# Two-layer graph network with attention: residual adds on VectorE, later signs, earlier reciprocals, a later row of means

## Chip, cores and metric

The kernel runs on one core of a Trainium2 chip. The metric is the device time in microseconds of one execution. All arithmetic is float32.

## What is computed

The reference takes x (16 batches of 1024 nodes with 256 features) and an adjacency matrix of 1024 x 1024, and applies two layers, each followed by a layer norm over the features. The second layer is the one that the change concerns:

```python
x = layernorm(x + L0(x, adj, ...))        # two matrix products with batch norms
# L1, per batch, fea = x transposed (C x N)
c = mean(x over features)                  # one number per node
A = abs(abs(sigmoid(c[None,:] - c[:,None]) - 0.5) - 0.5) * 2.0
Wg = adj * (A + A.T) * 0.5
g = relu(einsum('cn,nm->cm', fea, Wg) * para)
q = heads(g.T);  k, v = heads(x @ kv_w)    # 4 heads of 64
attn = softmax(q @ k.T * scale)
x = layernorm(x + attn @ v)
```

The abs(abs()) expression is computed by the kernel as 1 + tanh(-|d|/2) on the difference d of two nodes' means. For odd rows it takes tanh(-d/2) and sets the sign bit, which gives the same.

## The kernel before

The first layer takes the time up to about 820 us of the profile. From there `fast()` runs the second layer as one software pipeline over the 16 batches. It is cut into 256 attention steps, 16 to a batch. A step computes the scores of two blocks of keys for a pair of heads and 512 queries (`scores`, L771), their exponentials on ScalarE (`exps`, L783), adds these into a running sum on VectorE (`sums`, L789 and L792), and multiplies them with the values (`attend`, L807). After the last key block ScalarE and VectorE put the two halves of the product together (`ot`, L818 and L819), and SyncE stores it to DRAM.

Between groups of four steps stand the other pieces of work, each a small function that issues instructions on several engines in program order:

- `dens` (L834, L836): TensorE sums the running sums `acc` over partitions into `pd`; ScalarE copies that to `dt`. `recips` (L845, L847): TensorE transposes `dt` into `pr`, VectorE takes reciprocals into `RD`.
- `fetch_o` loads the stored attention output back in 32 x 32 blocks (`ob`, L860); `finish_a` transposes it on VectorE (L876), multiplies by the reciprocals (L880) and adds the residual `x1` (L885), on GpSimd for all batches but the last. `finish_s` takes layer-norm statistics of the sum on VectorE (`st_z`, `mv_z`) and the scale on GpSimd (`rs_z`, `nm`). `finish_b` applies them on ScalarE (L901) and stores the rows.
- For the next batch but one: `load`, `bn2_q` (GpSimd, L603), `rows` (VectorE, L607 and L608), `ln1_a` (statistics), `ln1_b` (VectorE, L628), `put_x1`, `get_x1` and `x1_v` (a transpose by way of DRAM), `means` (VectorE, L667 and L669), and `crow`, which spreads the row of means over all partitions: TensorE transposes it (`pc`, L684), ScalarE copies it (L686), SyncE writes it to DRAM and reads it back into 128 partitions (L687, L688).
- For the next batch: `gate` (ScalarE's abs and tanh into `wg`, L696 to L701; VectorE's sign, L698, and the product with the adjacency, L705), `keys`, `values` and `graph` (TensorE, L720, L731, L745) and `queries` (L753, L754).

A table `at` says in which half step-group each piece is issued. `arrange` puts the pieces of one half in order: pieces with short TensorE work are spread among the long ones (`keys`, `values`, `graph`), others go in by the rank in the tuple `order`, and gates are spread among the rest or put ahead. The first `sums` of a group is issued after the last short piece (`behind`). Each engine works through its own queue in this order, and an instruction that waits holds up all behind it.

Of the kernel before, what the change touches and what calls it, by code (L numbers as in the profile page):

```python
# [11 lines left out]
OP = mybir.AluOpType  # L12
# [10 lines left out]
def gnn_norm_attention_kernel(  # L23
# [16 lines left out]
    nc = tc.nc  # L40
    B, N, C = x.shape
# [82 lines left out]
    with ExitStack() as l0:  # L124
# [32 lines left out]
        with ExitStack() as ph1:  # L157
# [9 lines left out]
            for i in range(0, NT, 2):  # L167
                t = hp.tile([P, 2, N], F32, tag="h", name=f"A{i}")
# [22 lines left out]
            KB = FB // P  # L191
# [6 lines left out]
            for h in range(NH):  # L198
                rows = range(h * KB, (h + 1) * KB)
# [243 lines left out]
        with ExitStack() as ph2:  # L443
# [74 lines left out]
            for k, pair in enumerate(pairs):  # L518
# [4 lines left out]
                if not ahead:  # L523
                    for j in range(LDP):
                        load(0, j)
                    for j in range(LDP, NT // 2):
                        t = accp.tile([P, 2, FB], F32, tag="acc", name=f"first{j}")
# [17 lines left out]
    def ln_stats(sm, r, name):  # L545

        n = r.shape[1]
        mv = sm.tile([P, n, 2], F32, tag="mv", name=f"mv_{name}")
        for a in range(n):
            st = sm.tile([P, 6], F32, tag="st", bufs=2, name=f"st_{name}_{a}")  # L550
            nc.vector.bn_stats(st, r[:, a, :])  # L551
            nc.vector.bn_aggr(mv[:, a, :], st)
        rs = sm.tile([P, n], F32, tag="rs", name=f"rs_{name}")
        rsqrt(rs, mv[:, :, 1], EPS)
        return mv, rs
# [4 lines left out]
    def fast():  # L560
      with ExitStack() as fx:
# [15 lines left out]
        x1s, x1Ts, css, crows, mvs, wgs = {}, {}, {}, {}, {}, {}  # L577
# [113 lines left out]
        def wg_a(b, i):  # L691
            t = wgp.tile([P, N], F32, tag="wg", name=f"wg_{b}_{i}")
            wgs[b, i] = t
            if i % 2:

                nc.scalar.activation(t, crows[b], AF.Tanh, bias=hcs[b][:, i : i + 1], scale=-0.5)  # L696
                ti = t.bitcast(mybir.dt.int32)
                nc.vector.tensor_scalar(ti, ti, -(2**31), None, op0=OP.bitwise_or)  # L698
            else:
                nc.scalar.activation(t, crows[b], AF.Abs, bias=css[b][:, i : i + 1], scale=-1.0)  # L700
                nc.scalar.activation(t, t, AF.Tanh, scale=-0.5)  # L701

        def wg_b(b, i):
            t = wgs[b, i]
            nc.vector.scalar_tensor_tensor(t, t, 1.0, adj_sb[:, i, :], op0=OP.add, op1=OP.mult)  # L705

        def gate(b, i):
# [88 lines left out]
        def by_pe(b, hf):  # L796
            return b == B - 1 and hf == NH - 1
# [41 lines left out]
        R = {}  # L839
        KB = FB // P  # L840
# [24 lines left out]
        def finish_a(b, j):  # L865
            hf, k = divmod(2 * j, KB)
            pool_r = (rp, "r") if b < B - 1 else (x1p, "x1")
            r = pool_r[0].tile([P, 2, C], F32, tag=pool_r[1], name=f"r_{b}_{j}")
            if by_pe(b, hf):
                p = ps_t.tile([P, 2, C], F32, tag="t", name="pf")  # L870
                for a in range(2):
                    for pair in range(NP):
                        nc.tensor.transpose(p[:, a, ts(pair, P)], OT[b, hf, pair][:, ts(k + a, P)], ident)
            else:
                p = r
                nc.vector.transpose(  # L876
                    r.rearrange("p a c -> p (a c)"), OB.pop((b, j)).rearrange("p a c -> p (a c)")
                )
            rd = RD[:, b * NT + 2 * j : b * NT + 2 * j + 2, :].rearrange("p a h -> p (a h)")
            nc.vector.tensor_mul(  # L880
                r.rearrange("p a (h d) -> p (a h) d", h=HEADS),
                p.rearrange("p a (h d) -> p (a h) d", h=HEADS),
                rd.unsqueeze(2).to_broadcast([P, 2 * HEADS, HD]),
            )
            (nc.gpsimd if b < B - 1 else nc.vector).tensor_add(r, r, x1s.pop((b, j)))  # L885
            R[b, j] = r

        def finish_s(b, j):
            r = R[b, j]
            mv, rs = ln_stats(sm, r, f"z{b}_{j}")  # L890
            nm = sm.tile([P, 2], F32, tag="nm", name=f"nm_{b}_{j}")
            for a in range(2):
                nc.gpsimd.tensor_scalar(
                    nm[:, a : a + 1], mv[:, a, 0:1], rs[:, a : a + 1], -1.0, op0=OP.mult, op1=OP.mult
                )
            R[b, j] = (r, rs, nm)
# [42 lines left out]
        def put(w, t, f, *a):  # L939
            at.setdefault(w * NC + t, []).append((f, a))  # L940
# [4 lines left out]
        for b in range(B):  # L945

            for hf in range(NH):
                t = (hf + 1) * (NC // NH)
                put(b, t, dens, b, hf)
                put(b, t + 1, recips, b, hf)  # L950
                for k in range(KB // 2):
                    put(b, t + k, fetch_o, b, hf * (KB // 2) + k)
                    put(b, t + 1 + k, finish_a, b, hf * (KB // 2) + k)
                    put(b, t + 1 + k, finish_s, b, hf * (KB // 2) + k)
                    late = 0 if b == B - 1 else 1
                    if b == B - 1 and hf == 0:
                        late = NC - t - 2 - k
                    put(b, t + 2 + k + late, finish_b, b, hf * (KB // 2) + k)
            if b == 0:
                continue  # L960

            put(b - 2, 2, begin, b)
            for j in range(NT // 2):
                put(b - 2, j, load, b, j)
                put(b - 2, j + 1, bn2_q, b, j)
                put(b - 2, j + 2, rows, b, j)
                put(b - 2, j + 2, ln1_a, b, j)
                put(b - 2, j + 3, ln1_b, b, j)
                if b == 1:
                    put(b - 2, j + 4, x1_t, b, j)  # L970
                    continue
                put(b - 2, j + 3, put_x1, b, j)
                put(b - 2, 5 + j // 2 * 2, get_x1, b, j)
                put(b - 2, min(6 + j, NC), x1_v, b, j)
            put(b - 2, NC - 2, means, b)
            put(b - 2, NC - 1, crow, b)

            i = 0
            for t, n in enumerate(WG):
                for i in range(i, i + n):  # L980
                    put(b - 1, t, gate, b, i)
                i += 1
            kv = [(keys, (b, c, h)) for h in range(NH) for c in range(CT)]
            kv += [(values, (b, j)) for j in range(0, NT, 2)]
            for t, n in enumerate(KV):
                for _ in range(n):
                    f, a = kv.pop(0)
                    put(b - 1, t, f, *a)
            m = 0
            for t, n in enumerate(QG):  # L990
                for m in range(m, m + n):
                    put(b - 1, NC - len(QG) + t, graph, b, m)
                m += 1
# [3 lines left out]
        nsteps = B * NS  # L997


        order = (dens, recips, x1_t, finish_a, fetch_o, finish_b, x1_v, rows, ln1_a, ln1_b, put_x1, get_x1, finish_s, means, load, crow)  # L1000
        rank = {f: k for k, f in enumerate(order)}
        short = (dens, recips, x1_t, crow)

        def is_short(fa):
            f, a = fa
# [2 lines left out]
        long = (keys, values, graph)  # L1008

        def spread(few, many):  # L1010

            res, done = [], 0
            for k, fa in enumerate(few):
                upto = len(many) * (k + 1) // (len(few) + 1)
                res += many[done:upto] + [fa]
                done = upto
            return res + many[done:]

        def arrange(pieces):
            first = [fa for fa in pieces if fa[0] is dens]  # L1020
            gates = [fa for fa in pieces if fa[0] is gate]
            many = [fa for fa in pieces if fa[0] in long]
            first += [fa for fa in pieces if fa[0] is bn2_q]
            few = [fa for fa in pieces if fa not in first + gates + many]
            few.sort(key=lambda fa: rank.get(fa[0], len(rank)))
            few_pe = [fa for fa in few if is_short(fa)]
            order = spread(many, few_pe) if len(many) < len(few_pe) else spread(few_pe, many)
            if few_pe and many and order[0][0] in long:
                order.remove(few_pe[0])
                order.insert(0, few_pe[0])  # L1030

            for fa in few:
                if not is_short(fa):
                    at_ = 0
                    for k, o in enumerate(order):
                        if o[0] in rank and rank[o[0]] <= rank.get(fa[0], len(rank)):
                            at_ = k + 1
                    order.insert(at_, fa)
            if any(fa[0] is graph for fa in many):
                return first + gates + order  # L1040
            return first + spread(order, gates)

# [22 lines left out]
        def gate0(i):  # L1067
            wg_a(0, i)
            wg_b(0, i)
# [81 lines left out]
        )  # L1151

    flag = fast()


# [153 lines left out]
```

## Time and profile before

| | |
|---|---|
| median of 3 runs | 2532.7 us (2531.0 to 2536.48) |
| profiled execution | span 2531.8 us, the run 2533.6 us |
| TensorE clock granted | 0.995 |
| one batch in the steady part | 105.1 us |
| GpSimd's residual adds, L885 | 60, 1.27 us each |
| VectorE's sign operations, L698 | 64, 0.69 us each |

The profile gives the busy time of each engine over the span. The wait lists say, for an engine, which instruction waited, what ended the wait, how long in all, how often, and the longest. In a timeline each row has the start, the duration, the engine, the line and tile, and in brackets the idle time of the engine just before and what ended it. PE is TensorE, DVE VectorE, ACT ScalarE, POOL GpSimd, SP SyncE.

### The profile page before, as it was taken

How to read it: one execution, taken by the hardware profiler on the slowest of the kernel's cores; microseconds unless marked ns; L12 is line 12 of the kernel's file. 1: busy time of each engine (PE TensorE's matmuls, PEld its weight loads, DVE VectorE, ACT ScalarE, POOL GpSimd, SP SyncE). 2: the span in 40 equal slices, each digit the busy share in tenths (PEclk: the TensorE clock that was granted, in tenths of full speed). 3: DMA queues.
4: the chain of work that ended last, by engine and by line, in shares of the span. 5: the costliest groups of instructions: out<-in, count | busy, mean ns of one | idle time of the engine just before them, and what ended most of it. 6: DMA issues, size and time to landing. Idle time of an engine off the chain costs nothing.

```text
span 2531.8 us, 33526 instructions
## 1 busy us (share of the span) xinstructions
PE 2445.6 (97%) x12341; PEld 1025.0 (40%) x12341; DVE 1791.6 (71%) x2716; ACT 1037.6 (41%) x1325; POOL 786.3 (31%) x766
## 2 busy tenths in 40 slices
PE   8999999998998999999999999999999999999997
PEld 4444444443443433343343433434334343343432
DVE  5545554556767677877878778787787887878657
ACT  2000000004453446364563645636446364463644
POOL 2222322232565222331423314233142331423122
PEclk9999999999999999999999999999999999999999
DMA  3122212230885223333333233332333324323111
GB/s 133 67 89 94 100 68 93 88 126 28 289 312 183 59 46 72 84 71 79 74 73 87 64 85 72 70 88 63 83 75 69 88 63 89 71 67 88 26 42 44
DMA packets 545770, 225.71 MB, mean 89 GB/s; under 512 B 388680, under 2 KB 533696, under 8 KB 538432
## 3 DMA queue, kind: packets, MB, share of 16 engines
q1 hardware_dynamic: 545600, 223.50, 33.2%
q8 instruction: 99, 1.62, 0.3%
q14 instruction: 71, 0.58, 0.1%
HBM read 129.52 MB, written 93.91 MB: 88 GB/s over the span
## 4 chain that ended last, share of the span: by engine, by line
PE 41%; DVE 19%; issue 5%; ACT 5%; DMA 3%; POOL 2%; SPq 1%; DVEq 0%; POOLq 0%; ACTq 0%
PE s L771 11%; PE o L807 10%; PE pg L745 10%; DVE acc L792 8%; PE po L483 7%; DVE wg L705 2%; DVE x L628 2%; DMA yt<-yT 1%; PE pv L731 1%; PE pd L834 1%; ACT wg L700 1%; ACT wg L696 1%; POOL yt L603 1%; ACT wg L701 1%; DVE st_z L551 1%
## 5 line engine op out<-in xcount | busy, mean ns | idle before, releaser
L783 ACT ACTIVATE e<-s 128x1024 f32<-128x1024 f32 x512 | 496.5, 1022 | 619.1 <-PE s L771 565.0
L792 DVE TENSOR_TENSOR acc<-acc,e 128x1024 f32<-128x1024 f32 x384 | 508.5, 1324 | 79.9 <-ACT e L783 50.4
L771 PE MATMUL s<-qT,kT 64*64 64x512 f32 x4096 | 492.1, 595 | 18.6 <-ACT e L783 17.9
L807 PE MATMUL o<-e,v 64*64 64x512 f32 x4096 | 494.7, 589 | 0.0
L745 PE MATMUL pg<-wg,x 128*128 128x512 f32 x960 | 427.2, 595 | 0.0
L603 POOL TENSOR_TENSOR yt<-yt,stq 128x512 f32<-128x512 f32 x120 | 169.4, 1412 | 459.2 <-DMA yt<-yT 304.9
L807 PEld LDWEIGHTS o<-e,v 64*64 64x64 f32 x4096 | 160.9, 133 | 288.6 <-issue 271.1
L771 PEld LDWEIGHTS s<-qT,kT 64*64 64x64 f32 x4096 | 147.7, 133 | 314.5 <-issue 266.6
L745 PEld LDWEIGHTS pg<-wg,x 128*128 128x128 f32 x960 | 177.6, 190 | 219.7 <-issue 211.3
L885 POOL TENSOR_TENSOR r<-r,x 128x512 f32<-128x512 f32 x60 | 76.4, 1274 | 451.5 <-issue 380.3
L102 ACT COPY u<-pa 128x512 f32<-128x512 f32 x15 | 8.8, 586 | 475.3 <-PE pa L307 475.3
L705 DVE SCALAR_TENSOR_TENSOR wg<-wg,adj_sb 128x1024 f32<-128x1024 f32 x128 | 157.6, 1251 | 7.7 <-ACT wg L701 7.5
L307 PE MATMUL pa<-AhT,x 128*128 128x512 f32 x360 | 161.8, 592 | 0.0
L720 PE MATMUL pk<-x1T,kvw 128*128 128x512 f32 x256 | 118.4, 606 | 1.3 <-DVE x1T L664 1.3
L731 PE MATMUL pv<-kvw,x1T 128*128 128x256 f32 x512 | 117.1, 382 | 0.0
L338 PE MATMUL ph<-agg,SW 128*128 128x512 f32 x240 | 112.8, 592 | 0.0
L731 PEld LDWEIGHTS pv<-kvw,x1T 128*128 128x128 f32 x512 | 96.0, 190 | 31.5 <-issue 16.2
L307 PE MATMUL pa<-T,sx 128*128 128x512 f32 x240 | 107.9, 592 | 0.0
L307 PEld LDWEIGHTS pa<-AhT,x 128*128 128x128 f32 x360 | 68.4, 190 | 86.1 <-issue 86.1
L483 PE MATMUL po<-hL,SV 128*128 128x512 f32 x224 | 98.4, 592 | 0.0
L819 DVE TENSOR_TENSOR ot<-o,ot 128x512 f32<-128x512 f32 x64 | 44.0, 687 | 74.7 <-ACT ot L818 74.7
L467 ACT ACTIVATE hL<-hL,t,s 128x512 f32<-128x512 f32 x112 | 79.7, 802 | 25.0 <-DMA hL<-h 25.0
(195 smaller groups left out, 3035.8 us busy)
## 6 DMA issues: line engine op xcount, KB each, us to landing
h<-hT SPq DMA_DIRECT2D x28, 1024.0 KB, 4.4
hL<-h SPq DMA_DIRECT2D x28, 1024.0 KB, 9.6
x<-in_x_dram SPq DMA_DIRECT2D x16, 1024.0 KB, 7.3
yT<-y SPq DMA_DIRECT2D x64, 256.0 KB, 2.6
out_dram<-r SPq DMA_DIRECT2D x64, 256.0 KB, 2.4
xr<-in_x_dram SPq DMA_DIRECT2D x62, 256.0 KB, 3.0
o<-ot SPq DMA_DIRECT2D x62, 256.0 KB, 2.3
ob<-o SPq DMA_DIRECT2D x248, 64.0 KB, 2.2
```

What stands on the lines that cost most here:

```text
L307: nc.tensor.matmul(p, xs[n][:, k, :], bs[n][:, k, :], start=(k == 0), stop=(k == KN - 1))
L338: nc.tensor.matmul(p, ws[n][:, ts(f, P)], bs[n], start=True, stop=True)
L483: nc.tensor.matmul(p, ws[n][:, k, :], bs[n][:, k, :], start=(k == 0), stop=(k == KF - 1))
L603: nc.gpsimd.tensor_tensor(y, y, sc, op)
L705: nc.vector.scalar_tensor_tensor(t, t, 1.0, adj_sb[:, i, :], op0=OP.add, op1=OP.mult)
L720: nc.tensor.matmul(p, kvw[:, k, ts(c, P)], x1Ts[b][:, k, ts(h, FB)], start=(k == 0), stop=(k == CT - 1))
L731: nc.tensor.matmul(p[:, ts(a, C)], x1Ts[b][:, k, ts(j + a, P)], kvw[:, k, C:], start=(k == 0), stop=(k == CT - 1),)
L745: nc.tensor.matmul(pg[b], x1s[b, k // 2][:, k % 2, ts(c, P)], wgs[b, k][:, ts(h, FB)], start=(k == 0), stop=(k == NT - 1))
L771: nc.tensor.matmul(t[r * HD : (r + 1) * HD, h, :], kTs[b, pair][h * HD : (h + 1) * HD, ts(2 * cb + r, HD)], qTs[b, pair, hf][h * HD : (h + ...
L783: nc.scalar.activation(E[g, a], S.pop((g, a)), AF.Exp)
L792: nc.vector.tensor_add(ACC[b, hf, pair], ACC[b, hf, pair], E[g, a])
L807: nc.tensor.matmul(O[b, hf, pair][r][h * HD : (h + 1) * HD, :], vs[b][r * HD : (r + 1) * HD, cb, pair * P + h * HD : pair * P + (h + 1) * HD],
```

## The change

Four things are done. The residual add of a finished row moves from GpSimd to VectorE for all batches, and its statistics follow it in the same piece, so `finish_s` is gone. The sign bit of an odd gate row is set where its product with the adjacency is issued, which is two rows later. The reciprocals are issued in the same half as the denominators, ahead of the second long piece, and the first sums of the group after them. The row of means, `crow`, is issued last in its half, behind the graph pieces, and no longer counts as a short piece.

```diff
         def wg_a(b, i):
...
                 nc.scalar.activation(t, crows[b], AF.Tanh, bias=hcs[b][:, i : i + 1], scale=-0.5)
-                ti = t.bitcast(mybir.dt.int32)
-                nc.vector.tensor_scalar(ti, ti, -(2**31), None, op0=OP.bitwise_or)
...
         def wg_b(b, i):
             t = wgs[b, i]
+            if i % 2:
+                ti = t.bitcast(mybir.dt.int32)
+                nc.vector.tensor_scalar(ti, ti, -(2**31), None, op0=OP.bitwise_or)
             nc.vector.scalar_tensor_tensor(t, t, 1.0, adj_sb[:, i, :], op0=OP.add, op1=OP.mult)
...
-            (nc.gpsimd if b < B - 1 else nc.vector).tensor_add(r, r, x1s.pop((b, j)))
-            R[b, j] = r
-
-        def finish_s(b, j):
-            r = R[b, j]
+            nc.vector.tensor_add(r, r, x1s.pop((b, j)))
             mv, rs = ln_stats(sm, r, f"z{b}_{j}")
...
                 put(b, t, dens, b, hf)
-                put(b, t + 1, recips, b, hf)
+                put(b, t, recips, b, hf)
...
                     put(b, t + 1 + k, finish_a, b, hf * (KB // 2) + k)
-                    put(b, t + 1 + k, finish_s, b, hf * (KB // 2) + k)
...
-        short = (dens, recips, x1_t, crow)
+        short = (dens, recips, x1_t)
...
-            few = [fa for fa in pieces if fa not in first + gates + many]
+            alone = [fa for fa in pieces if fa[0] in (recips, crow)]
+            few = [fa for fa in pieces if fa not in first + gates + many + alone]
...
             if any(fa[0] is graph for fa in many):
-                return first + gates + order
-            return first + spread(order, gates)
+                order = gates + order
+            else:
+                order = spread(order, gates)
+
+            k = ([n for n, fa in enumerate(order) if fa[0] in long] + [len(order)] * 2)[1]
+            order[k:k] = [fa for fa in alone if fa[0] is recips]
+            return first + order + [fa for fa in alone if fa[0] is crow]
```

More of the change, by code (lines that the diff above doesn't have):

```diff
@@ L997, in fast @@
         nsteps = B * NS
-        order = (dens, recips, x1_t, finish_a, fetch_o, finish_b, x1_v, rows, ln1_a, ln1_b, put_x1, get_x1, finish_s, means, load, crow)
+        order = (dens, recips, x1_t, finish_a, fetch_o, finish_b, x1_v, rows, ln1_a, ln1_b, put_x1, get_x1, means, load, crow)
         rank = {f: k for k, f in enumerate(order)}
-        short = (dens, recips, x1_t, crow)
+        short = (dens, recips, x1_t)
         def is_short(fa):
```

## The prediction

> **What bounds the kernel now.** I read the page's first part, then TensorE's waits, then one batch in the windows view, then the timelines of TensorE, ScalarE, VectorE, GpSimd and SyncE over that batch. The busy line of the page:
>
> ```profile
> PE 2445.6 (97%) x12341; PEld 1025.0 (40%) x12341; DVE 1791.6 (71%) x2716; ACT 1037.6 (41%) x1325; POOL 786.3 (31%) x766
> ```
>
> TensorE is idle for 2531.8 - 2445.6 = 86 us, and its matmuls are not touched by the change. So only its waits can be won or made. The rows of its wait list (total, times, longest) that the change can reach:
>
> ```profile
> PE s L771 <- ACT e L783: 17.9, 15, 3.1
> PE pd L834 <- DVE acc L792: 10.8, 15, 1.8
> PE pc L684 <- DVE cs L667: 10.2, 14, 0.7
> ...
> PE pr L845 <- ACT dt L836: 2.1, 3, 0.7
> ```
>
> They sum to 41.0 us. One batch (105.1 us, the distance of two pc transposes) has TensorE at 102.78, and its timeline shows where the other 2.3 are:
>
> ```profile
> 1383.20:1488.30 105.10, 102.78 (x649) 41.41 (x649) 82.31 (x126) 55.15 (x67) 32.91 (x36) 1.00 0.35 76
> ```
>
> ```profile
> 1383.41 0.27 PE L684 MATMUL pc<-ident,cs 128*8 128x128 f32 x1 [0.73 <-DVE cs L667]
> ...
> 1418.25 2.00 PE L771 MATMUL s<-qT,kT 64*64 64x512 f32 x16 [1.00 <-ACT e L783]
> ...
> 1458.26 1.05 PE L834 MATMUL pd<-acc,ones 128*32 128x512 f32 x4 [0.58 <-DVE acc L792]
> ```
>
> 0.73 + 1.00 + 0.58 = 2.31: the list is complete. I call the four stretches of a batch, each work pieces and then four attention steps, A (from 1402.7: denominators, keys, six gate rows), B (1428.8: two gate rows, values, ten graph pieces), C (1456.6: denominators, ten graph pieces) and D (1482.4: twelve graph pieces, crow).
>
> The waits of A and B-to-C have different owners. In A ScalarE works without a gap from 1403.79 (dt) to 1419.1; it decides the 1.00. The 0.58 is VectorE's, which from 1418.01 to 1458.81 has no gap, and which came late into that stretch because of two waits. VectorE in A, B and C:
>
> ```profile
> 1408.56 0.69 DVE L698 TENSOR_SCALAR wg<-wg 128x1024 int32<-128x1024 int32 x1 [3.28 <-ACT wg L696]
> ...
> 1418.01 0.43 DVE L551 BATCH_NORM_STATS2 st_z<-r 128x6 f32<-128x256 f32 x1 [3.30 <-POOL r L885]
> ...
> 1421.95 9.36 DVE L792 TENSOR_TENSOR acc<-acc,e 128x1024 f32<-128x1024 f32 x6
> 1431.23 0.68 DVE L819 TENSOR_TENSOR ot<-o,ot 128x512 f32<-128x512 f32 x1
> ...
> 1440.19 1.30 DVE L608 TENSOR_TENSOR x<-x,xr 128x512 f32<-128x512 f32 x1
> ...
> 1449.03 9.18 DVE L792 TENSOR_TENSOR acc<-acc,e 128x1024 f32<-128x1024 f32 x6
> 1458.13 0.68 DVE L819 TENSOR_TENSOR ot<-o,ot 128x512 f32<-128x512 f32 x1
> ```
>
> **What the Trainium skill says.** "VectorE: DVE Perf Modes", in the section on the TRN2 errata, gives an fp32 tensor_tensor add as (N+151)/0.96 ns: 691 for 512 elements. The trace has this very add on VectorE for the last batch, 4 at 692 ns. "GPSIMD Engine Reference", Engine selection, calls such an op about twice as slow on GpSimd; the trace: 1268 against 692, 1.8 times. "SBUF — State Buffer", in the section on the two separate sides, says that a GpSimd op and a VectorE op with two SBUF inputs exclude each other for a whole instruction. The trace agrees: the add of L608 at 1440.19 took 1.30 instead of 0.69, since GpSimd's residual add ran from 1439.67 to 1440.94.
>
> **The change, part by part**, on this batch.
>
> *Residual adds.* 60 GpSimd adds of 1.27 us (76.4 us of an engine that is 31% busy) become 60 VectorE adds of 0.69, 41.5 us, four a batch or 2.8. Taken away: VectorE's waits for GpSimd's r, 45.8 us before st_z and 20.0 before L607 by its list, 4.4 a batch, and the lockout of some 0.6 where an add met a VectorE op. The statistics now follow at once, so those of the finished row come before rows and ln1_a, and GpSimd's rs_z before rs_a.
>
> *Signs.* The 64 sign operations (0.69 each) stay. What goes is the 55.1 us in which VectorE stood before a tanh just issued. Row 5's sign moves from A to B.
>
> *Reciprocals.* The four transposes (0.60 us) and the reciprocal (0.25) come after the first keys or graph piece following dens instead of after a whole half, and the first sum of the stretch (1.16) with them, ahead of the finished row. The transposes wait for ScalarE's dt. With nothing between, the last batch shows 0.69 to 0.71 us of TensorE's waiting. In C one graph piece (two matmuls, 10 take 4.46 for five pieces, so 0.87) lies between: 0.71 - 0.87 is below 0, so no wait. In A a keys piece (four matmuls, 1.8) covers it. Bounds 0 and 0.71 a time; I take 0.
>
> *Finished row after it.* Its transposed load, ob, is no longer covered. In A it is issued until 1408.3; in the last batch a load issued until 1457.0 let its reader start at 1458.79, so 1410.1 here. Queued behind this wait on VectorE are signs, gate rows and sums. The readers of the gate rows are B's graph pieces, from 1434 on.
>
> *Row of means.* The pc transpose (0.27) goes behind the twelve graph pieces, with its ScalarE copy (0.26) and two SyncE transfers (0.33 and 0.34 of issue, 3.8 to landing). VectorE's means move later too: the sum (1.18), the add, and statistics ahead give about +2 us, to about 1385.4 in D, still before the transpose at 1388.8. On SyncE the rewritten rows wait for that VectorE order; x1T's last block is freed some 3 us later, so the eight loads of L652 and crow end about 3 to 5 us later, and crow lands by about 1397 (bounds: unchanged 1393.5, or 1398.5). Its first reader starts at 1405.27; x1_v reads at 1404. Both slacks are over 6 us, so I cost them at nothing. Behind crow on SyncE is only the ot store at 1404.1.
>
> **The sum.** pc: all 10.2 us gone. pd, by walking VectorE through the new order. In A: ot add and two x1_v to 1405.3; reciprocal about 1406.3; sum 1407.5; gate row 0 to 1408.7; ob until 1410.1 to 1410.4; transpose, product, add 1412.4; statistics 1413.6; sign and row 1 1415.3; row 2 1416.4; sign and row 3 1418.2. The six sums start there instead of 1421.95, and are then limited by the last exponentials (1423.9 to 1424.9): done at about 1427.4 instead of 1431.2. VectorE then waits for ScalarE's ot (1429.5), so it enters B 1.7 us early, not 3.8. In B it pays row 5's sign (0.61) and the add (0.63), and gets back the lockout at L608 (0.6) and a gap of 0.2 before st_z: the six sums start at 1449.0 - 1.7 + 1.24 - 0.8 = 1447.7 and end at 1456.9. The last denominators need them at 1458.26 - 0.58 = 1457.7. So this wait vanishes with 0.8 to spare: 10.8 - 1.82 - 1.60 (the two of the last batch) = 7.4 us over 13 batches. In the last batch two rows of b = 14 each give 1.44 of wait for 0.69 of add, 0.75 each: 1.5 of the 1.82; the 1.60 stays. The 17.9 on s stay, since ScalarE's work between dt and the exponentials is the same. Total 10.2 + 7.4 + 1.5 = 19.1 us. The profiled span was 2531.8, within 1 of the run's 2533.6 and of the 2532.7 median; 2532.7 - 19.1 = 2513.6, and I say 2514.
>
> Costs not seen, from both sides: the transposes for the reciprocals 0 to +10 (14 times 0.71); pd 0 to -7.4; the PSUM buffers in A and C, which are handed out in another order, 0 to +5 (an o tile in A looks held up by 0.7 now, 2.60 for 1.90, behind key copies; the s wait after it would absorb a gain); pc 0 to -10.2; GpSimd's lockouts falling elsewhere, -2 to +3.
>
> **Rivals.** *Half a gain.* VectorE gains nothing net in B, or the transposes wait; then only pc and the tail are won, 10.2 + 1.5, perhaps less some us: 2519 to 2527. For it: the stretch from 1418 to 1458 is gapless and four adds are put into it and before it. Against: the waits removed are larger than the adds.
>
> *Slower: VectorE becomes the bound.* VectorE's stretch B has only one wait of 0.2 to lose, while it gets 1.24 us more. If it does not come into B early, the pd wait grows from 0.58 to 1.8, 14 times +1.2 = +17; if lockouts remain as well, each of 60 adds costing 1.3, that is another +8; less pc's 10.2 and with the reciprocals' wait up to +10: 2540 to 2557. It decides at ScalarE's ot of stretch A, 1429.5: VectorE must have its six sums done by then. I have 1427.4; an ob that lands over 2 us later, or another wait of that size behind it, turns it.
>
> *No effect.* The won pieces come back in A as more of the wait on s. Against: A's wait is counted from its own denominators, so it moves along with TensorE. 2528 to 2537. That the edits change no order at all is excluded by the diff, as each moves an instruction on its queue.
>
> **How the numbers follow.** Forecast 0.60, with its own range 2508 to 2518; half a gain 0.20; no effect 0.06; slower 0.14. About 0.2% (5 us) is what a measurement of this kernel can tell from no change. So faster 0.80, same 0.06, slower 0.14. The range 2507 to 2528 takes in the first two cases with the bounds above and leaves out the 0.20 of the others.
>
> **What would show it.** No row for TensorE's pc waiting on cs, and pd on acc at 2 to 3 us in all; pr on dt no more than 2 to 4; s on e still near 18. Period of a batch 103.8 instead of 105.1. VectorE: no st_z or L607 waiting on r, no L698 on wg; new waits of r L876 on ob, about 1.5 us twice a batch. VectorE busy within +20 and +42, GpSimd down by about 76. The prediction is wrong if the batch stays at 105, or if pd or pr on TensorE's list exceeds 15 us.

## The result and the profile after

The changed kernel takes 2518.57 us (median of 6 runs, 2517.56 to 2521.39) against 2534.59 for the kernel before in the same comparison: a ratio of 0.9938, 95% interval 0.9926 to 0.9951, so 16 us less (12 to 19). The forecast was 2514, within 2507 to 2528, for 19.1 us. So the measured time lies in the range, half a microsecond above the forecast's own part of it (2508 to 2518).

The busy line of the page, and the rows of TensorE's waits that answer to those shown before (us in total, times, longest):

```profile
PE 2437.9 (97%) x12341; PEld 1024.0 (41%) x12341; DVE 1847.9 (73%) x2776; ACT 1037.3 (41%) x1325; POOL 694.2 (28%) x706
```

```profile
PE s L772 <- ACT e L784: 26.9, 15, 3.1
...
PE pd L835 <- DVE acc L793: 4.8, 9, 1.6
...
PE pr L846 <- ACT dt L837: 2.1, 3, 0.7
```

The waits of pc on cs in the batches are gone from the list, pd on acc has fallen from 10.8 to 4.8, pr on dt has not moved. VectorE has 56 us more of work: 41.5 are the adds, and 17 are gate products and signs that take longer (L705 before, 157.6 to 169.7; L698 before, 44.3 to 49.2), while the adds of L608 take 8.5 less (50.0 to 41.5). GpSimd has 92 less. The wait on s grew by 9.0 us, yet the o products' busy time fell by nearly as much (494.7 to 486.1): a wait that lay inside the row of o before, as the prediction suspected, is now listed at s.

TensorE's timeline of one batch, the same places as those shown of the kernel before:

```profile
1384.63 0.27 PE L684 MATMUL pc<-ident,cs 128*8 128x128 f32 x1
...
1398.72 1.07 PE L835 MATMUL pd<-acc,ones 128*32 128x512 f32 x8
1399.72 1.98 PE L721 MATMUL pk<-x1T,kvw 128*128 128x512 f32 x4
...
1414.32 2.01 PE L772 MATMUL s<-qT,kT 64*64 64x512 f32 x16 [1.70 <-ACT e L784]
...
1452.69 1.05 PE L835 MATMUL pd<-acc,ones 128*32 128x512 f32 x4
1453.99 1.05 PE L835 MATMUL pd<-acc,ones 128*32 128x512 f32 x4 [0.25 <-DVE acc L793]
1454.98 1.13 PE L746 MATMUL pg<-wg,x 128*128 128x512 f32 x2
```

The rows of C in the kernel before:

```profile
1456.63 1.05 PE L834 MATMUL pd<-acc,ones 128*32 128x512 f32 x4
1458.26 1.05 PE L834 MATMUL pd<-acc,ones 128*32 128x512 f32 x4 [0.58 <-DVE acc L792]
1459.25 4.56 PE L745 MATMUL pg<-wg,x 128*128 128x512 f32 x10
```

The reader should look here at starts, not at brackets. Undisturbed denominators, eight matmuls, are followed by the next piece after 1.00 us (1398.72 to 1399.72; 0.99 ahead of graph pieces). In C it takes 2.29 us (1452.69 to 1454.98), so 1.30 are lost while the bracket says 0.25. The last four, issued late and alone, take as long as all eight side by side (1453.99 to 1454.98 is 0.99), so their whole delay after the first four is lost; the bracket counts only what is left of it after the 1.05 that the first four are drawn long. In the kernel before it was 2.62 us, 1.63 lost, not 0.58. I took the losses of all batches from starts in this way. "C loss" is the sum of what the denominators of the 15 stretches with graph pieces take beyond 0.99 (the first and the last lose nothing), "A to C" and "C to A" are the distances of the denominators in a batch, the latter less C's loss (us). "Signs back" and the rows below it are experiments that follow:

```
kernel            C loss   A to C   C to A less loss   last matmul's end
before             20.95    53.97        49.5               2522.05
changed            16.75    53.97        48.6               2505.63
crow only          18.70    53.97        48.6               2509.89
residual only      10.98    53.97        49.9               2520.26
signs only         21.41    53.97        49.5               2522.91
reciprocals only   19.72    53.97        49.5               2524.18
changed, signs back 8.15    53.97        48.6               2496.29
half of bn2         0.92    53.97        48.6               2489.12
five gate rows     16.92    52.93        48.6               2491.61
  signs 1, 3       15.04    52.93        48.6               2489.07
  signs 0, 1, 3    13.96    52.39        48.6               2477.54
```

Before to changed: 14 times 0.89 in C to A (the row of means) is 12.4, 4.2 in C, and 1.3 at b = 15's first denominators (4.60 to 3.31 from the first to the transposes): 17.9. The profiles agree: from the first denominators of the second layer to the end of the last matmul the changed kernel takes 17.7 us less. These denominators came 1.3 us later in it, so its last matmul ends 16.4 earlier.

### The profile page after: what moved, and what is told of

Same layout as the page of the kernel before. It is cut to its first block, busy times and chain, and to the rows that moved or that the text cites. A ratio compares the mean times of both kernels' runs of the same rounds, so it can differ in the third digit from the quotient of the medians.

```text
span 2515.8 us, 33531 instructions
## 1 busy us (share of the span) xinstructions
PE 2437.9 (97%) x12341; PEld 1024.0 (41%) x12341; DVE 1847.9 (73%) x2776; ACT 1037.3 (41%) x1325; POOL 694.2 (28%) x706
## 3 DMA queue, kind: packets, MB, share of 16 engines
q8 instruction: 99, 1.62, 0.3%
## 4 chain that ended last, share of the span: by engine, by line
PE 49%; DVE 15%; ACT 7%; issue 2%; DMA 1%; SPq 0%; DVEq 0%; POOL 0%; ACTq 0%; POOLq 0%
PE pg L746 13%; PE s L772 13%; PE o L808 12%; PE po L483 7%; DVE acc L793 5%; DVE wg L706 2%; ACT wg L696 2%; ACT wg L698 1%; PE pv L732 1%; PE pd L835 1%; ACT wg L699 1%; ACT kT L724 1%; DVE st_a L551 1%; ACT e L784 1%; DVE x L607 1%
## 5 line engine op out<-in xcount | busy, mean ns | idle before, releaser
L772 PE MATMUL s<-qT,kT 64*64 64x512 f32 x4096 | 491.8, 595 | 27.7 <-ACT e L784 26.9
L808 PE MATMUL o<-e,v 64*64 64x512 f32 x4096 | 486.1, 589 | 0.0
L603 POOL TENSOR_TENSOR yt<-yt,stq 128x512 f32<-128x512 f32 x120 | 181.3, 1511 | 446.9 <-DMA yt<-yT 185.3
L66 POOL TENSOR_SCALAR rs_z<-mv_z 128x2 f32<-128x2 f32 x64 | 28.2, 441 | 662.9 <-DVE mv_z L552 653.3
L706 DVE SCALAR_TENSOR_TENSOR wg<-wg,adj_sb 128x1024 f32<-128x1024 f32 x128 | 169.7, 1345 | 14.0 <-ACT wg L699 10.6
L732 PEld LDWEIGHTS pv<-kvw,x1T 128*128 128x128 f32 x512 | 96.0, 190 | 31.5 <-issue 16.5
```

The lines of the kernel that those rows point to most:

```text
L603: nc.gpsimd.tensor_tensor(y, y, sc, op)
L732: nc.tensor.matmul(p[:, ts(a, C)], x1Ts[b][:, k, ts(j + a, P)], kvw[:, k, C:], start=(k == 0), stop=(k == CT - 1),)
L772: nc.tensor.matmul(t[r * HD : (r + 1) * HD, h, :], kTs[b, pair][h * HD : (h + 1) * HD, ts(2 * cb + r, HD)], qTs[b, pair, hf][h * HD : (h + ...
L808: nc.tensor.matmul(O[b, hf, pair][r][h * HD : (h + 1) * HD, :], vs[b][r * HD : (r + 1) * HD, cb, pair * P + h * HD : pair * P + (h + 1) * HD],
```

## The experiments

Ratios are to the kernel before, run on the same chip. The changed kernel was not run again beside them, so a difference to it is taken from the two ratios.

**One edit at a time.** Only the row of means (`crow` in `alone`, put at the half's end, out of `short`):

```diff
-        short = (dens, recips, x1_t, crow)
+        short = (dens, recips, x1_t)
...
-                return first + gates + order
-            return first + spread(order, gates)
+                return first + gates + order + alone
+            return first + spread(order, gates) + alone
```

> Of the four edits only the row of means, issued last in its half. My theory: TensorE's 14 waits of pc on cs (10.2 us) vanish and nothing else moves: 10 us faster than the kernel before, pd on acc stays near 10.8 us and s on e near 17.9. Rival (the gain comes from VectorE's lead, and a later crow only hands the wait on to the next scores or to the first gate row): within 3 us of before.

Measured: 2522.54 us, ratio 0.9955 (0.9942 to 0.9969), 11 us faster; pd at 8.6 and s at 17.8. The theory holds but for the 2.2 us by which pd fell too; the rival falls.

Only the residual adds:

```diff
-            (nc.gpsimd if b < B - 1 else nc.vector).tensor_add(r, r, x1s.pop((b, j)))
-            R[b, j] = r
...
-        def finish_s(b, j):
-            r = R[b, j]
+            nc.vector.tensor_add(r, r, x1s.pop((b, j)))
...
```

> Only the residual adds on VectorE, with the statistics behind them. My theory: VectorE's waits for r go, pd on acc falls from 10.8 to 4 to 7 us, pc on cs stays at 10.2: 4 to 7 us faster than before. Rival (VectorE is the bound, 41.5 us more of work outweigh the waits): pd on acc at 20 us or more, 8 us or more slower.

Measured: 2528.81 us, ratio 0.9978 (0.9969 to 0.9987), 5.6 us faster. The waits show that the total hides two opposite things:

```profile
PE pc L684 <- DVE cs L667: 15.6, 14, 1.1
...
PE pd L834 <- DVE acc L792: 2.7, 5, 1.6
```

C's loss falls by 10.0 us, more than I expected, but pc on cs rises from 10.2 to 15.6: an added 0.69 us now stands ahead of `means`, and 0.39 more a batch shows in C to A. In the whole change the later crow hides that (48.6 in both), so the edit is worth more in company than alone. The kernel with the other three edits and without the later signs, below, bears this out: it gains 24 us, where these three alone sum to 18.

Only the signs (the two lines moved from `wg_a` to `wg_b`):

> Only the signs two rows later. My theory: VectorE's 55 us of waiting before the sign turn into waits for the reciprocals' transposes and for r, and row 5's sign is paid later in the stretch, so TensorE's waits stay: within 2 us of before. Rival (these waits feed the pd wait): pd on acc falls by 4 us or more, and the time with it.

Measured: 2538.46 us, ratio 1.0010 (1.0002 to 1.0019), 2.5 us slower, a little more than I allowed; pd 11.0. The wait list of VectorE says where its 55 us before the sign went:

```profile
DVE st_z L551 <- POOL r L886: 52.4, 18, 4.2
...
DVE wg L706 <- ACT wg L699: 40.6, 18, 3.2
```

They became waits for the even rows' tanh (7.5 us before) and longer ones for r (43 to 46 us in the kernel before and in those with the crow or the reciprocals alone). The waits for the reciprocals' transposes, which I had named as well, stayed at 37. The rival falls.

Only the reciprocals (`put(b, t, recips, b, hf)`, ahead of the second long piece):

> Only the reciprocals next to the row sums, with the first sums of a stretch behind them. My theory: the transposes find dt ready behind one long piece, so no new wait of TensorE, and 0.7 us a batch moves from the o products to the wait on s: within 2 us of before. Rival (TensorE now waits for ScalarE's copy): pr on dt at 8 us or more and that much slower.

Measured: 2534.07 us, ratio 0.9996 (0.9987 to 1.0004), no difference; pr on dt 2.1, s on e 27.0. As expected. The four edits alone, -11.4, -5.6, +2.5 and -1.0, sum to -15.5 us, and the change has -16. That the sums agree is chance: the next experiment shows that the signs cost far more in company than alone. The wait on s is 27.0 with the residual adds alone too, so each of these two edits by itself brings it to light.

**Signs back, in the changed kernel.**

```diff
         def wg_a(b, i):
...
                 nc.scalar.activation(t, crows[b], AF.Tanh, bias=hcs[b][:, i : i + 1], scale=-0.5)
+                ti = t.bitcast(mybir.dt.int32)
+                nc.vector.tensor_scalar(ti, ti, -(2**31), None, op0=OP.bitwise_or)
...
         def wg_b(b, i):
             t = wgs[b, i]
-            if i % 2:
-                ti = t.bitcast(mybir.dt.int32)
-                nc.vector.tensor_scalar(ti, ti, -(2**31), None, op0=OP.bitwise_or)
```

> The changed kernel with the sign operation set back to where the tanh is issued; the other three edits stay. The kernel with only the sign moved was 0.1% slower than the kernel before. My theory: in the changed kernel too the later sign is worth nothing to TensorE, as what VectorE no longer waits at the sign it waits for the loaded rows, and row 5's sign is paid in the stretch ahead of the last denominators: 0 to 3 us faster than the changed kernel, pd on acc at 2 to 5 us. Rival (together with the early reciprocals the later sign is what lets VectorE come early): 4 us or more slower than it, pd on acc above 8 us.

Measured: 2509.35 us, ratio 0.9904 (0.9889 to 0.9919): 9 us faster than the changed kernel, beyond the 3 I allowed. The direction was mine, the size was not. VectorE in stretches A and B of this kernel, which begin at 1395.89 and 1422.02:

```profile
1401.81 0.69 DVE L698 TENSOR_SCALAR wg<-wg 128x1024 int32<-128x1024 int32 x1 [3.29 <-ACT wg L696]
...
1404.79 0.70 DVE L876 STREAM_TRANSPOSE r<-ob 128x512 f32<-128x512 f32 x1
...
1409.45 2.35 DVE L705 SCALAR_TENSOR_TENSOR wg<-wg,adj_sb 128x1024 f32<-128x1024 f32 x2
...
1413.46 9.33 DVE L792 TENSOR_TENSOR acc<-acc,e 128x1024 f32<-128x1024 f32 x6
1422.74 0.69 DVE L819 TENSOR_TENSOR ot<-o,ot 128x512 f32<-128x512 f32 x1
...
1441.36 9.37 DVE L792 TENSOR_TENSOR acc<-acc,e 128x1024 f32<-128x1024 f32 x6
```

and the same places of the changed kernel, whose stretches begin at 1398.72 and 1424.84:

```profile
1402.18 0.26 DVE L848 RECIPROCAL RD<-pr 128x16 f32<-128x16 f32 x1 [0.83 <-PE pr L846]
...
1406.44 0.71 DVE L877 STREAM_TRANSPOSE r<-ob 128x512 f32<-128x512 f32 x1 [1.62 <-DMA ob<-o]
...
1410.42 3.94 DVE L706 SCALAR_TENSOR_TENSOR wg<-wg,adj_sb 128x1024 f32<-128x1024 f32 x2
...
1416.16 9.21 DVE L793 TENSOR_TENSOR acc<-acc,e 128x1024 f32<-128x1024 f32 x6
1425.56 0.69 DVE L820 TENSOR_TENSOR ot<-o,ot 128x512 f32<-128x512 f32 x1 [0.18 <-ACT ot L819]
...
1444.64 9.30 DVE L793 TENSOR_TENSOR acc<-acc,e 128x1024 f32<-128x1024 f32 x6
```

With the signs in place VectorE waits 3.29 us in A, and still starts A's six sums at +17.57 (counted from the start of the stretch), the changed kernel at +17.44; both enter B with ot at +0.72. So the wait removed in A is worth nothing here: in the changed kernel VectorE waits 0.83 us for the transposes and 1.62 for ob instead, and its pair of rows takes 3.94 us instead of 2.35. In B, where VectorE has no slack, row 5's sign comes on top: the six sums begin at +19.34 without it, +19.80 with it. C's loss is 8.15 against 16.75 us: 8.6 us, or 0.66 in each of the 13 stretches that lose anything, where one sign takes 0.69.

**GpSimd's lockouts.**

```diff
-            for k, op in enumerate((OP.mult, OP.add)):
-                sc = stq[:, k, :].unsqueeze(1).unsqueeze(3).to_broadcast([P, 2, C // Q, Q])
-                nc.gpsimd.tensor_tensor(y, y, sc, op)
+            sc = stq[:, 0, :].unsqueeze(1).unsqueeze(3).to_broadcast([P, 2, C // Q, Q])
+            nc.gpsimd.tensor_tensor(y, sc, sc, OP.subtract)
```

> The changed kernel with one GpSimd operation of the two per loaded block: it leaves out the first layer's contribution from the second batch on (it subtracts a tile from itself instead of scaling and shifting). It takes away half of GpSimd's long operations, and no operation of VectorE. My theory: VectorE is late by GpSimd's lockouts, so pd on acc falls from 4.8 to 2.2 us (what the last batch has), and the two gate rows that took 3.9 us together in the first stretch take 2.5: 2 to 4 us faster than the changed kernel. Rival (the added work itself makes VectorE late): pd on acc stays at 4 to 5 us.

Measured: 2500.00 us, ratio 0.9863 (0.9847 to 0.9878), 19 us faster than the changed kernel (the last matmul of the profile ends 16.5 earlier); pd 2.1 on the list, C's loss from 16.75 to 0.92. VectorE's six sums of A took 8.51 instead of 9.21 us, those of B 8.63 instead of 9.30, and the pair of rows 2.36 instead of 3.94:

```profile
1405.88 2.36 DVE L705 SCALAR_TENSOR_TENSOR wg<-wg,adj_sb 128x1024 f32<-128x1024 f32 x2
...
1410.03 8.51 DVE L792 TENSOR_TENSOR acc<-acc,e 128x1024 f32<-128x1024 f32 x6
1420.59 0.69 DVE L819 TENSOR_TENSOR ot<-o,ot 128x512 f32<-128x512 f32 x1 [2.05 <-ACT ot L818]
...
1439.54 8.63 DVE L792 TENSOR_TENSOR acc<-acc,e 128x1024 f32<-128x1024 f32 x6
```

GpSimd's operations that run beside these in the changed kernel:

```profile
1409.85 3.44 POOL L603 TENSOR_TENSOR yt<-yt,stq 128x512 f32<-128x512 f32 x2 [27.95 <-DVE mv_z L552]
...
1448.49 3.04 POOL L603 TENSOR_TENSOR yt<-yt,stq 128x512 f32<-128x512 f32 x2 [2.06 <-DMA yt<-yT]
```

VectorE does the same operations, and its wait list has no row for the blocks that GpSimd prepares in either kernel, so the lengthening of VectorE's operations by GpSimd's is shown to carry nearly all that was left of the loss in C. The direction agrees with the exclusion that "SBUF — State Buffer" of the Trainium skill describes in its section on the two separate sides: the pair of rows took 3.94 us beside two GpSimd operations, and 2.36 where the one that is left had ended before it. The lead of 2.05 us that VectorE now has at the end of A is lost in the wait for ot: it enters B at +0.72, as in the changed kernel. The sizes expected came from the list (2 to 4 us) and were again too small.

**Transposes at once** (recips directly behind dens, no long piece between):

```diff
-            order[k:k] = [fa for fa in alone if fa[0] is recips]
-            return first + order + [fa for fa in alone if fa[0] is crow]
+            return [fa for fa in first if fa[0] is dens] + [fa for fa in alone if fa[0] is recips] + [fa for fa in first if fa[0] is not dens] + order + [fa for fa in alone if fa[0] is crow]
```

> The changed kernel with the reciprocals' transposes directly behind the denominators, with no long piece between. My theory: each of the 30 costs TensorE 0.71 us of waiting for dt, in the stretches with graph pieces in full (14 times, 10 us), while in those with key pieces the wait on s shrinks by as much: pr on dt at 22 us, s on e at 17 us, 8 to 12 us slower than the changed kernel. Rivals: the wait is paid in both stretches, 20 us slower; or ScalarE's copy is hidden anyway, within 2 us.

Measured: 2528.44 us, ratio 0.9979 (0.9970 to 0.9988), 10 us slower than the changed kernel.

```profile
PE pr L846 <- ACT dt L837: 22.3, 32, 0.7
PE s L772 <- ACT e L784: 16.7, 15, 3.1
```

Both numbers as expected: one long piece does hide dt, and in A any wait of TensorE is paid out of the one on s.

**Five gate rows in A**, and products one row behind:

```diff
-        WG = (3, 3, 2)
+        WG = (3, 2, 3)
...
-            for k in range(i - 2, i + 1) if i == NT - 1 else (i - 2,):
+            for k in range(i - 1, i + 1) if i == NT - 1 else (i - 1,):
```

> The changed kernel with five gate rows instead of six in the stretch with the keys and three in the next, and the products one row behind instead of two, so that VectorE has four rows' products in the first stretch as before. My theory: ScalarE's gapless stretch alone sets the wait on s, so one tanh less (1.05 us) brings it from 26.9 to 11 to 13 us; pd on acc may rise by up to 5: 9 to 15 us faster than the changed kernel. Rival (VectorE, which now waits for tanh rows just issued, becomes late): pd on acc above 15 us and no gain.

Measured: 2501.57 us, ratio 0.9867 (0.9852 to 0.9882), 18 us faster than the changed kernel, somewhat over the range expected. s on e is 11.5 us, A to C 52.93 instead of 53.97: the 1.04 is one tanh, 14.6 us in 14 batches, and the last matmul of the profile ends 14.0 earlier. C's loss stays at 16.9 and pd on acc at 5.2, so the rival falls.

**Rows 5 and 7 without a sign operation**, on top of that (`if i in (1, 3)` for `if i % 2` in both functions):

> The kernel with five gate rows in the first stretch, and in it rows 5 and 7 no longer by tanh and sign bit but by abs and tanh as the even rows (the same result), so that VectorE has no sign operation ahead of the last denominators and ScalarE two activations more in a stretch where it idles 8 us. My theory: what is left of the pd wait, counted from start to start (the changed kernel: 16.7 us over the 14 stretches with graph pieces), is VectorE's time in the stretch before it, and falls one for one by 2 x 0.61 a batch: to under 4 us, and the kernel is 10 to 16 us faster than that with five rows alone. Rival (VectorE there is held by transfers or GpSimd, not by its own work): under 4 us faster.

Measured: 2502.45 us, ratio 0.9873 (0.9858 to 0.9888), no gain over the run before; C's loss 15.04. My theory fell. In the batch shown the 1.22 us taken off VectorE in B come back as waits for ScalarE's longer rows and as longer sums (10.03 us, with five rows alone 9.30), beside which more of GpSimd's work now runs:

```profile
1424.20 1.23 DVE L706 SCALAR_TENSOR_TENSOR wg<-wg,adj_sb 128x1024 f32<-128x1024 f32 x1 [0.18 <-ACT wg L699]
1426.32 1.23 DVE L706 SCALAR_TENSOR_TENSOR wg<-wg,adj_sb 128x1024 f32<-128x1024 f32 x1 [0.90 <-ACT wg L699]
...
1438.03 10.03 DVE L793 TENSOR_TENSOR acc<-acc,e 128x1024 f32<-128x1024 f32 x6
```

**Row 0 with a sign operation**, on top (`if i in (0, 1, 3)`):

> As the run before, and row 0 by tanh and sign bit, which takes one activation (1.06 us) off ScalarE in the stretch with the keys and gives VectorE 0.6 us there, at a place where it waits for the loaded rows. My theory: the wait on s that was 0.66 a batch goes to 0 in 14 batches, 7 to 10 us faster than the run before, as long as VectorE still ends its sums of that stretch in time; if it does not, the pd wait takes back up to 0.6 a batch. Rival (something else than ScalarE sets the last 0.66): no gain on s.

Measured: 2490.74 us, ratio 0.9826 (0.9812 to 0.9839), 12 us faster than the run before, somewhat over the range expected, and the fastest kernel of the study: 1.7% under the kernel before. s on e is 1.0 us in all, A to C 52.39. That is 0.54 a batch, 7.6 us in 14; C's loss fell by another 1.1, and the opening before the first denominators, where row 0 stands too, is 1.7 shorter. The last matmul ends 11.5 earlier; most of the remaining 1.1 lies in the first layer (0.7), which the edit doesn't touch.

**Adds back on GpSimd, statistics behind them.**

```diff
-            nc.vector.tensor_add(r, r, x1s.pop((b, j)))
+            (nc.gpsimd if b < B - 1 else nc.vector).tensor_add(r, r, x1s.pop((b, j)))
```

> The changed kernel with the residual adds back on GpSimd, the statistics directly behind them as in the change. My theory: VectorE now stands behind GpSimd's add at every row (1.4 us at least, 3 and more where GpSimd is at its long operations), so TensorE's wait at the last denominators grows by 1 to 2 us a batch: 10 to 30 us slower than the changed kernel, VectorE's wait for r at 90 us or more. Rival (the add's place does not matter, since 41 us more of VectorE's work make up for it): within 4 us.

Measured: 2572.95 us, ratio 1.0157 (1.0143 to 1.0170), 54 us slower than the changed kernel. The theory's direction, and a greater size than its range: C's loss is 57.7 us, C to A is 10.7 longer in all, and VectorE's list has

```profile
DVE st_z L551 <- POOL r L886: 135.1, 60, 6.1
```

In the kernel before that wait was 45.8. There the statistics came later in the order, which probably kept it small; no run here takes that difference alone.

## Why the prediction was right, by its own steps

*The total* is nearer than its terms. Against 19.1 us expected the kernel gained 16. The row of means brought more than its term and the pd wait less, and that these two errors have opposite signs is luck. "Half a gain", which began at 2519, is not told apart from the forecast by the total; its reason, that VectorE gains nothing net in B, is close to what the late signs made of it (C's loss is 16.75 us with them and 8.15 without, against 20.95 before).

*What bounds the kernel* was read rightly: TensorE's waits only, ScalarE in A, VectorE in B. The distance A to C is 53.97 us in both kernels, and only ScalarE's own work (five rows, row 0) shortened it.

*The row of means* was right: 10.2 us expected from the list, 12.4 by starts (0.89 a batch, not 0.73; "the list is complete" did not hold). The later SyncE transfers cost nothing. In the changed kernel crow was issued at 1389.17, by 3.4 us nearer to A than before, as forecast; it lands about 3.7 us after its issue, and its first reader started at 1401.34.

*The reciprocals* at 0 were right, and the bound of 0.71 a time was shown by taking the long piece away. The new wait for ob is there, 60.1 us over 31 times on VectorE, 1.62 in A and 1.79 in C of the batch shown (about 1.5 was forecast), and in that batch no wait of TensorE follows from it.

*The pd term was mis-sized.* The step said "this wait vanishes with 0.8 to spare", 7.4 us and 1.5 in the last batch. Measured: 4.2 and 1.3, and 16.75 us of loss in C stayed. Two things were wrong in it. It took the wait from the list, 0.58 a batch, where starts give 1.63. And its walk through B came out 0.9 short: VectorE came into B at +0.72 as worked out, but the six sums began at +19.80, not +18.9. B of the kernel before and of the changed one:

```profile
1434.10 0.69 DVE L698 TENSOR_SCALAR wg<-wg 128x1024 int32<-128x1024 int32 x1
1434.70 3.49 DVE L705 SCALAR_TENSOR_TENSOR wg<-wg,adj_sb 128x1024 f32<-128x1024 f32 x3
...
1438.84 0.69 DVE L880 TENSOR_TENSOR r<-r,RD 128x512 f32<-128x512 f32 x1
1439.45 0.70 DVE L607 STREAM_TRANSPOSE x<-yt 128x512 f32<-128x512 f32 x1
```

```profile
1428.43 0.69 DVE L705 TENSOR_SCALAR wg<-wg 128x1024 int32<-128x1024 int32 x1
1429.15 2.36 DVE L706 SCALAR_TENSOR_TENSOR wg<-wg,adj_sb 128x1024 f32<-128x1024 f32 x2
1431.43 0.69 DVE L705 TENSOR_SCALAR wg<-wg 128x1024 int32<-128x1024 int32 x1
1432.15 1.23 DVE L706 SCALAR_TENSOR_TENSOR wg<-wg,adj_sb 128x1024 f32<-128x1024 f32 x1
...
1434.04 0.69 DVE L881 TENSOR_TENSOR r<-r,RD 128x512 f32<-128x512 f32 x1
1434.76 0.69 DVE L886 TENSOR_TENSOR r<-r,x 128x512 f32<-128x512 f32 x1
1435.49 0.43 DVE L551 BATCH_NORM_STATS2 st_z<-r 128x6 f32<-128x256 f32 x1
```

From start to start the inserted sign and add cost 0.72 and 0.73, not 0.61 and 0.63. The sign of row 7 and the product ahead of the add, which took 0.60 and 0.61 before, take 0.72 each now that the operation behind them reads what they have just written. The lockout at L608 did go, but the gap of 0.2 to be taken back stands in no wait list of this stretch of the kernel before, and nothing came of it. In A the margin of 2 us was used up by lockouts, which stood under "falling elsewhere, -2 to +3" and were not placed.

*The signs* were costed as part of a lead gained in A. The wait that they removed in A came back at the transposes and at ob, and a lead over ScalarE's ot is worth nothing (2.05 us of it, with half of bn2, changed nothing at B's entry); the kernel with the signs left in place is 9 us faster. The prediction named both facts, the entry at 1.7 rather than 3.8 and the 0.61 paid in B, and did not draw from them that this edit loses.

*The rival "VectorE becomes the bound"* did not come, but was near: its point of decision, the sums of A done by ot at +0.72, was met at +0.53, by 0.2 us and not by the 2 worked out. Its "another +8" fits the 14 adds of B at 0.6 each, not the "each of 60 adds" of its words.

*The signs to look for*: no waits of pc on cs in the batches and none of VectorE for r, pr at 2.1, and a batch of 103.87 us (pc at 1384.63 and 1488.50) came as said. Missed were pd (4.8, for 2 to 3), s on e (26.9, for 18), VectorE's added work (56, for 20 to 42) and GpSimd's (92 less, for 76): the lengthening of VectorE's operations and the wait hidden in o were not in the account.

## What to carry to other kernels

Before a wait of one engine is taken away, follow that engine to the next place where it waits anyway: work moved from ahead of such a place to behind it costs time there, and a wait removed ahead of it may gain nothing. Measure what a wait costs the bounding engine from start to start of its instructions and not from the idle time in a list, and test each edit of a bundle also by taking it out of the whole.

## What the runs showed of the hardware

A VectorE operation with two inputs in SBUF was lengthened by concurrent GpSimd work: two products of 1024 elements took 2.36 us with half the GpSimd work and 3.94 with all of it, and six sums 8.63 against 9.30. Which operations it meets shifts with the order: in the change the adds of L608 got shorter (50.0 to 41.5 us in all) and the gate products longer (157.6 to 169.7). Halving GpSimd's long operations (181 us busy in the whole kernel) made this kernel 19 us faster, though GpSimd itself was idle for 72% of the span.

Two smaller facts: a VectorE operation of 0.69 us was followed by the next after 0.60 or 0.61 us where that one did not need its result, and after 0.72 or 0.73 where it did. And eight matmuls of 32 columns each took TensorE 1.00 us to its next piece, four of them alone 0.99.
